# One core, four layers: values joined to the output weights in layer 0, softmax transposes in one row, and another pace of sampling in layer 1

## The chip, the core and the metric

The kernel runs on one core of a Trainium2 chip. A core has a matrix engine (PE), a vector engine (DVE), a scalar engine (ACT), a general one (POOL), one that mostly issues DMAs (SP), and DMA queues. The engines run side by side, each through its own list of instructions in order, and wait for each other by semaphores. The metric is the device time of one execution in microseconds; the median of several runs counts. All data is 32-bit float.

## What is computed

The input `x` has two images of 512 channels with 32 x 32 points (1024). Four layers follow each other:

```python
# layer 0: attention of 1024 points over 64 sampled keys, 8 heads of 64
sim = einsum("bhid,bhjd->bhij", qh, kh) + bias      # bias: a small MLP of point and key
attn = softmax(sim)
out = einsum("bhij,bhjd->bhid", attn, vh)
x = x + einsum("bchw,oc->bohw", out, out_w) + out_b
x = x + mlp_w2 @ gelu(mlp_w1 @ bn(x) + b1) + b2     # 512 -> 2048 -> 512
# layer 1: d = normalised depthwise + pointwise convolution of the lower channels
off = conv(d, off_w)                                # 9 taps, an (y, x) offset each
dc = sum over taps of dc_w[tap] @ bilinear(d, tap + off)
x = x * d * sigmoid(layernorm(dc)) + x * g          # g: a gate from pooled channels
# layer 2: linear attention; layer 3: group norm, 8-head attention, projection
```

## The kernel before

**Order.** The order on PE is the order of the program; a tile scheduler orders DVE, ACT, POOL and SP by itself. `weave`, `some` and `next` step Python generators, and so mix stages by hand into PE's list: each `yield` is a place where another stage may be cut in. A tile pool with n buffers makes a new tile wait until the tile n before it has been read for the last time.

**Layer 0.** `queries_keys_values` makes queries, keys and values at the start. Keys and values are kept in block form, two heads to a block of 128 (`kbd`, `vbd`, L706 to L760). `biased_scores` then fills `simT` in 128 steps: hidden layers `h` (DVE L804, ACT L813), matmuls `ph` (L824), evictions `hi` and `lo` (L834 to L837), the last layer and the scores `sim` (L845), `store` (DVE L867). Pairs 0 to 3 of `simT` belong to image 0, pairs 4 to 7 to image 1. `softmax_values` works pair by pair: eight transposes `pt` (L909), maximum, subtraction, exponential, sum, reciprocal, product (L915 to L922), eight transposes `pb` back (L928), a copy `at` (ACT L934), the product with `vbd` (L940) and its copy into `simT` (DVE L943). `project` (L966) multiplies `simT` by `out_w`. For image 0 this runs alone; for image 1 it is woven into `mlp.run(0)`. `Mlp` has matmuls `ph` (L1026), gelu `h` (ACT L1034) and matmuls `acc` (L1015).

**Layer 1.** `Features` makes `x_pad` (memset on POOL L1079, copy on ACT L1084), the depthwise sums `dw` on DVE (L1092, L1096), `pd` (L1112), `d`, then `d_pad` (memset POOL L1139, copies ACT L1141), offsets `po` (L1153), `pos` (DVE L1165) and indices after `pp` (L1218). `Products` multiplies `d` by each of the 9 taps in 8 blocks: 72 steps per image, called "made" steps, each four matmuls `py` (L1291), a copy `y` (ACT L1299) and a DMA into a table in memory (SP L1300). `Samples` gathers from the finished tables: 72 pairs of indirect DMAs `got` per image (POOL L1343), with four additions `dfacc` on DVE each (L1354). `pools` lists the buffers for `got`; `due` takes one pair if the table of its tap is complete. `gate_image` applies the layer norm and the gate (transposes `pt` L1389, sigmoid `gated` ACT L1395, product L1398, `x_all` DVE L1400).

**How they are joined.** Image 0's products start in `mlp.run(1)`; its gathers go on with two buffers, then four beside image 1's features; `found` is the generator of features. Image 1's gathers go on three buffers while `gate_image(0)` steps once per made step, and on up to five afterwards while `linear.run(0)` and `group_norm_terms` step once per made step. `group_norm_terms` waits on DVE's `spread` for `pvar` (L1605).

**Layer 3.** `att.normalize` makes `h` (ACT L1663) from `x_all`; keys and queries `pq` (L1703) follow. `att.values(0)` makes `v` in 32 steps of one matmul `pv` (L1680), `BESIDE` of them per step of `linear.run(1)` (`pkv` L1550, `pa` L1564, evictions `x_all` L1573). `Attention.heads` then does logits `pl` (L1770), exponentials `e` (ACT L1866), transposes `pt` (L1820), weighing `po` (L1785).

## Time and profile before

| | us |
|---|---|
| median of three runs | 3969.76 |
| lowest and highest of them | 3967.2, 3973.1 |
| profiled execution | 3967.19 |
| its span, first to last instruction | 3965.4 |
| ACT's first exponential of the softmax, with its table (2114.55 to 2117.85) | 3.3 |
| POOL memset of d_pad (128 x 4624) | 3.96 |
| DVE add of a gather (128 x 512, mean of 560) | 0.748 |
| gather, issue to landing, median | 6.7 |
| table block, issue to landing, median | 5.5 |

A row of a timeline reads: start, duration, engine, line, operation, output and inputs with shapes, how often, and in brackets how long the engine sat idle before it and whose result it then had. A matmul of 32-bit floats shows as two records. The next view is of five stretches of the span (busy time of PE, PEld, DVE, ACT and POOL with counts, then granted clock, share of busy DMA engines and rate): the softmax of image 0, the features of image 1, the gate, the linear stage, the end of image 1's products.

```profile
2105.00:2152.00 47.00, 24.07 (x91) 14.14 (x92) 26.77 (x26) 9.57 (x10) 0.06 (x1) 0.78 0.53 221
2839.00:2985.00 146.00, 130.55 (x551) 57.83 (x550) 112.85 (x170) 28.87 (x46) 75.70 (x62) 0.92 0.85 305
2985.00:3125.00 140.00, 135.43 (x330) 60.43 (x328) 108.17 (x180) 29.39 (x52) 66.54 (x60) 0.97 0.90 331
3125.00:3240.00 115.00, 106.39 (x335) 52.06 (x334) 89.94 (x142) 19.59 (x34) 54.37 (x52) 0.96 0.80 292
3240.00:3313.00 73.00, 64.94 (x149) 28.23 (x147) 55.02 (x79) 12.31 (x21) 40.64 (x36) 0.97 0.96 365
```

### The profile page before, as it was taken

To read this page: it belongs to the slowest core of one execution; us is meant where nothing else is said; L and a number is where in the kernel's file an instruction comes from. 1 tells how busy PE (TensorE), PEld (TensorE's weight loads), DVE (VectorE), ACT (ScalarE), POOL (GpSimd) and SP (SyncE) were. 2 spreads that over 40 slices of the span, in tenths; PEclk is the share of its full clock that TensorE was granted. 3 is DMA by queue.
4 is the path that set the end of the run, shared out by engine and by line. 5 is a ranking of instruction groups with operands and counts; after the bars stand their busy time and mean duration, and the time that the engine had idled before them with its cause. 6 is when DMAs were issued, how large, how long until landed. Compare 5 with 4: busy or idle time off the path is not lost. (4 is left out here: it accounts for less than half of the span.)

```text
span 3965.4 us, 59982 instructions
## 1 busy us (share of the span) xinstructions
PE 3847.6 (97%) x25596; PEld 1498.6 (38%) x25596; DVE 2967.5 (75%) x3320; ACT 2536.3 (64%) x2858; POOL 340.7 (9%) x325
## 2 busy tenths in 40 slices
PE   7999999999999999999997999999999999999999
PEld 4322232222322222222333444444344444455555
DVE  7999999999999999999995114044577878666565
ACT  7999999999999999999992211211121212345544
POOL 0000000000000000000000000022354544000000
PEclk9999999999999999999998999999999999999999
DMA  3000000000000000000002000056788987000000
GB/s 106 2 22 22 22 23 1 22 22 23 17 7 22 23 22 3 21 22 22 1 1 106 0 0 24 18 177 198 259 289 320 336 300 256 1 1 11 1 19 25
DMA packets 90479, 274.66 MB, mean 69 GB/s; under 512 B 9140, under 2 KB 10804, under 8 KB 86884
## 3 DMA queue, kind: packets, MB, share of 16 engines
q0 software_dynamic: 42432, 154.39, 11.1%
q1 hardware_dynamic: 47780, 116.44, 8.2%
q8 instruction: 200, 3.28, 0.3%
q14 instruction: 67, 0.55, 0.0%
HBM read 228.59 MB, written 42.21 MB: 68 GB/s over the span
## 5 line engine op out<-in xcount | busy, mean ns | idle before, releaser
L824 PE MATMUL ph<-h,w_t 128*32 128x512 f32 x16384 | 1796.2, 593 | 15.3 <-ACT lo L834 7.0
L804 DVE TENSOR_TENSOR h<-ab 128x1024 f32<-128x1024 f32 x1024 | 1205.5, 1218 | 73.8 <-PE ph L824 72.7
L824 PEld LDWEIGHTS ph<-h,w_t 128*32 128x32 f32 x16384 | 528.8, 110 | 1257.3 <-issue 1079.2
L813 ACT ACTIVATE h<-h 128x1024 f32<-128x1024 f32 x832 | 870.4, 1066 | 45.5 <-DVE h L804 43.4
L837 DVE SCALAR_TENSOR_TENSOR hi<-lo,low_w,hi 128x1024 f32<-128x1024 f32 x512 | 654.6, 1278 | 30.0 <-ACT hi L836 29.3
L836 ACT ACTIVATE hi<-ph,size_b,size 128x1024 f32<-128x1024 f32 x512 | 620.5, 1212 | 15.6 <-PE ph L824 9.6
L834 ACT ACTIVATE lo<-ph,vec_t 128x1024 f32<-128x1024 f32 x512 | 571.2, 1116 | 2.4 <-PE ph L824 2.4
L1354 DVE SCALAR_TENSOR_TENSOR dfacc<-got,wts,dfacc 128x512 f32<-128x512 f32 x560 | 408.5, 748 | 214.9 <-DMA got<-table,idx 206.4
L1291 PE MATMUL py<-dc_w_t,d 128*128 128x512 f32 x1152 | 523.9, 610 | 23.1 <-ACT y L1299 23.1
L1299 ACT COPY y<-py 128x512 f32<-128x512 f32 x144 | 83.6, 584 | 478.3 <-PE py L1291 426.8
L1343 POOL DMA_INDIRECT got<-table,idx x288 | 319.9, 1111 | 501.1 <-DVE dfacc L1354 171.9
L1291 PEld LDWEIGHTS py<-dc_w_t,d 128*128 128x128 f32 x1152 | 221.1, 195 | 302.1 <-issue 269.5
L1866 ACT ACTIVATE e<-pl,m 128x1024 f32<-128x1024 f32 x128 | 143.5, 1121 | 217.1 <-DVE m L1858 217.1
L1858 DVE TENSOR_REDUCE m<-pl 128x1 f32<-128x1024 f32 x128 | 150.8, 1219 | 143.8 <-PE pl L1770 143.8
L845 PE MATMUL sim<-hi,w 128*32 128x512 f32 x2048 | 244.9, 592 | 1.8 <-DVE hi L837 1.8
L1026 PE MATMUL ph<-xn,mlp_w_t 128*128 128x512 f32 x512 | 229.6, 592 | 0.0
L1015 PE MATMUL acc<-h,mlp_w_t 128*128 128x512 f32 x512 | 229.3, 592 | 0.0
L1034 ACT ACTIVATE h<-ph,vec_t 128x512 f32<-128x512 f32 x64 | 44.0, 687 | 254.2 <-PE ph L1026 254.0
L1079 POOL MEMSET x_pad<- 128x1156 f32 x2 | 2.2, 1099 | 2061.5 <-PE ph L824 2061.5
L1820 PE MATMUL pt<-cst_t,e 128*128 128x128 f32 x1024 | 149.6, 279 | 4.8 <-DVE aT L1829 2.7
L1820 PEld LDWEIGHTS pt<-cst_t,e 128*128 128x128 f32 x1024 | 118.9, 142 | 92.4 <-issue 60.2
L1015 PEld LDWEIGHTS acc<-h,mlp_w_t 128*128 128x128 f32 x512 | 97.2, 190 | 122.0 <-issue 122.0
(233 smaller groups left out, 2472.3 us busy)
## 6 DMA issues: line engine op xcount, KB each, us to landing
table<-y SPq DMA_DIRECT2D x144, 256.0 KB, 5.5
ab<-feat_d SPq DMA_DIRECT2D x64, 512.0 KB, 4.4
dc_w_t<-in_dc_w_dram SPq DMA_DIRECT2D x18, 1024.0 KB, 6.2
mlp_w_t<-in_mlp_w_dram SPq DMA_DIRECT2D x2, 4096.0 KB, 16.8
got<-table,idx POOLq DMA_INDIRECT x288, 6.7
w_qkv_t<-in_w_qkv_dram SPq DMA_DIRECT2D x3, 1024.0 KB, 9.1
out_dram<-x_all SPq DMA_DIRECT2D x12, 256.0 KB, 2.0
x_all<-in_x_dram SPq DMA_DIRECT2D x4, 512.0 KB, 8.7
```

Of the source, the lines that this page charges most:

```text
L804: nc.vector.tensor_tensor(h1, at_x[:, k : k + 1, :].to_broadcast([128, 32, 32]), at_y[:, k, :].unsqueeze(2).to_broadcast([128, 32, 32]), A ...
L813: nc.scalar.activation(h1, h1, AF.Relu)
L824: nc.tensor.matmul(ph[32 * t : 32 * t + 32, half(n)], lhsT=w2[:, c0 : c0 + 32], rhs=pair[t // 2][:, half(n)], start=True, stop=True, skip_ ...
L834: nc.scalar.activation(lo, phs[0], AF.Relu, bias=b2_lo)
L836: nc.scalar.activation(hi, phs[1], AF.Relu, bias=size_b, scale=size)
L837: nc.vector.scalar_tensor_tensor(hi, lo, low_w, hi, ALU.mult, ALU.add)
L845: nc.tensor.matmul(sim[32 * t : 32 * t + 32, half(n)], lhsT=w3[:, 30 - j : 62 - j], rhs=sums[t][:, half(n)], start=(j == 0), stop=(j == 30 ...
L1015: nc.tensor.matmul(accs[oc], lhsT=self.w2[:, m, 128 * oc : 128 * oc + 128], rhs=hs[m], start=(m == 0), stop=(m == 15),)
L1291: nc.tensor.matmul(py, lhsT=f.d[:, cc, 128 * c : 128 * c + 128], rhs=w[:, cc, :], start=(cc == 0), stop=(cc == CC - 1),)
L1343: nc.gpsimd.indirect_dma_start(out=g[:, 2 * dy : 2 * dy + 2, :].rearrange("p s c -> p (s c)"), out_offset=None, in_=self.products.tables[f ...
L1354: self.net.nc.vector.scalar_tensor_tensor(acc, g[:, s, :], self.f.wts[:, c, k, s : s + 1], self.f.bias if (k, s) == (0, 0) else acc, ALU.mult,
L1820: nc.tensor.transpose(pt[:, 128 * c : 128 * c + 128], e[:, 128 * k : 128 * k + 128], ident)
```

## The change

- Values are made as block products `val`, one 128 x 128 block per pair of heads, by the loop that makes the keys. A new `projected` multiplies each block by the output weights once (`pm`, eight matmuls of 128 x 512, copied by ACT to `outv`); `project` uses `outv`, and the product with `vbd` and its copies go. Four `pm` stand ahead of image 0's projection, four behind it.
- The softmax of image 0 moves into `biased_scores`: the transposes of pairs 0 and 1 stand ahead of the last `last_layer`, those of pairs 2 and 3 behind it, then four `turn`, and `store` of the last pair comes last. `out_w` and `mlp_w1` are loaded at step 16 of the last pair, into the space of `q_pad`.
- Image 0's `Samples` get three buffers in the MLP of image 1, and one more afterwards; `due` is called there only while i < 30; image 1's features begin two made steps later.
- Image 1's `Samples` have two buffers until image 0's gate is done, then six. The gate takes two steps per made step; `linear.run(0)` steps in two of three made steps.
- `values(0)` of layer 3 takes 19 steps beside `linear.run(1)`, and the other 13 in `heads`, behind the first logits.

```diff
@@ -167,7 +163,7 @@
...
-        "vw": vw_stack,
+        "vw": _pair_blocks(np.asarray(i["L0_conv_vw"])),
...
@@ -292,46 +289,70 @@
         scores = ExitStack()
         sim_pool = net.pool(scores, "l0_sim", side="right")
         simT = sim_pool.tile([128, NP, HW], F32, name="simT", tag="simT")
-        vbd = sim_pool.tile([128, NP, 128], F32, name="vbd", tag="vbd")
+        val = sim_pool.tile([128, NP, 128], F32, name="val", tag="val")
+        room = ExitStack()
+        big = net.pool(room, "l0_q")
+        def new_room():
+            return big.tile([128, 4 * 2048 + CC * C], F32, name="room", tag="room")
         with ExitStack() as l0a:
             l0a.enter_context(net.tc.manual_schedule(engines={mybir.EngineType.PE}))
-            big = net.pool(l0a, "l0_q")
-            q_flat = big.tile([128, (NP * 36 + 6) * 34], F32, name="q_pad", tag="q_pad")
+            q_flat = new_room()[:, : (NP * 36 + 6) * 34]
...
             first = net.pool(l0a, "cpb_ab", 4)
-            parts = queries_keys_values(net, bn, simT, q_flat, q_pad, kbd, vbd, feat, first)
+            parts = queries_keys_values(net, bn, simT, q_flat, q_pad, kbd, val, feat, first)
...
-            biased_scores(net, q_pad, kbd, feat, w2, simT, first, parts)
+            def load_weights():
+                t = new_room()
+                w1 = t[:, : 4 * 2048].rearrange("p (k m) -> p k m", m=2048)
+                out_w = t[:, 4 * 2048 :].rearrange("p (k m) -> p k m", m=C)
+                nc.sync.dma_start(out=out_w, in_=net.ins["out_w"])
+                nc.sync.dma_start(out=w1, in_=net.ins["mlp_w1"])
+                return w1, out_w
+            w1, out_w = biased_scores(
+                net, q_pad, kbd, feat, w2, simT, first, parts, load_weights
+            )
         later.enter_context(net.tc.manual_schedule(engines={mybir.EngineType.PE}))
         dram = net.pool(later, "l1_dram", space=bass.MemoryType.DRAM)
         image0 = ExitStack()
-        with ExitStack() as l0b:
-            mlp = Mlp(net, l0b, s2)
-            out_w = net.load("out_w", net.pool(scores, "out_w", side="right"))
-            soft = net.pool(scores, "att_tmp", 2, side="right")
-            with ExitStack() as ctx:
-                ps = net.psum(ctx, "att_ps", 4)
-                for _ in softmax_values(net, 0, simT, vbd, soft, ps):
-                    pass
+        with room, ExitStack() as l0b:
+            mlp = Mlp(net, l0b, s2, w1)
+            soft = net.pool(scores, "att_tmp", side="right")
             mlp.open_psum(l0b)
             with ExitStack() as ctx:
                 ps = net.psum(ctx, "att_ps1", 1)
-                project(net, 0, simT, out_w, mlp.bank)
-                weave(mlp.run(0), softmax_values(net, 1, simT, vbd, soft, ps), 1, 3)
-                project(net, 1, simT, out_w, mlp.bank)
+                def two_banks(name):
+                    return ps.tile([128, HW], F32, name=name, tag="two")
+                def one(name, size):
+                    return soft.tile([128, size], F32, name=name, tag=name, bufs=2)
+                made = projected(net, val, out_w, soft, mlp.bank)
+                some(made, CC - 1)
+                outv = next(made)
+                project(net, 0, simT, outv, mlp.bank)
+                some(made, 99)
+                weave(mlp.run(0), Softmax(net, simT, one, two_banks).image(1), 1, 3)
+                project(net, 1, simT, outv, mlp.bank)
...
             with ExitStack() as ctx:
-                banks["turn"] = net.psum(ctx, "ft_ps", 2)
+                banks["turn"] = net.psum(ctx, "ft_ps", 2), "turn"
...
                 taken = None
@@ -339,18 +360,19 @@
                     some(found, FOUND[i] if i < len(FOUND) else 0)
                     if i == len(FOUND):
                         some(found, 99)
-                        sums0 = Samples(net, f0, products, own0, 2, side="right")
+                        sums0 = Samples(net, f0, products, own0, 3, side="right")
                         taken = sums0.run()
                     if i >= MADE:
                         for _ in range(2):
                             next(made)
-                            if taken is not None:
+                            if taken is not None and i < 30:
                                 sums0.due(taken)
...
             linear = Linear(net, l2)
             own1 = ExitStack()
             f1 = Features(net, 1, own1)
-            more = net.pool(own1, "df_more", 2)
-            sums0.pools += [more, more]
+            more = net.pool(own1, "df_more", 1)
+            sums0.pools += [more]
             found = f1.run(bank, True)
             for i, _ in enumerate(made):
-                some(found, 2)
+                if i > 1:
+                    some(found, 2)
                 if i % 4 < 3:
                     sums0.due(taken)
             some(found, 99)
             sums1 = Samples(net, f1, products, own1, 1)
-            sums1.pools += [more, more]
+            sums1.pools += [more]
             tmp = net.pool(own1, "df_tmp", 1)
             made = products.run(f1, turn)
             taken1 = sums1.run()
-            aside = None
+            aside, ctx2 = None, None
             for i, _ in enumerate(made):
-                if i == 62:
-                    sums1.pools = sums1.pools[:3]
                 if aside is None:
                     if next(taken, None) is None:
                         aside = gate_image(net, f0, sums0, tmp, bank)
                         wait = i + 4
-                else:
-                    sums1.due(taken1)
-                    if i >= wait and next(aside, None) == "gated":
-                        own0.close()
-                        ctx2 = ExitStack()
-                        extra = net.pool(ctx2, "df_extra", 2, side="right")
-                        sums1.pools += [extra, extra]
-                        linear.open(ctx2, side="right")
-                        aside = chain(
-                            linear.run(0, bank, kv_bank),
-                            group_norm_terms(net, linear.tmp, 0, bank),
-                        )
+                    continue
+                sums1.due(taken1)
+                if ctx2 is None and i >= wait:
+                    if next(aside) != "gated" and next(aside) != "gated":
+                        continue
+                    own0.close()
+                    ctx2 = ExitStack()
+                    linear.open(ctx2, side="right")
+                    extra = net.pool(own1, "df_extra", 4)
+                    sums1.pools += [extra] * 4
+                    aside = chain(
+                        linear.run(0, bank, kv_bank),
+                        group_norm_terms(net, linear.tmp, 0, bank),
+                    )
+                elif ctx2 is not None and i % 3 < 2:
+                    next(aside, None)
             for _ in aside:
                 next(taken1, None)
             ctx2.close()
@@ -415,9 +440,8 @@
                 values = att.values(0, turn)
                 for i, _ in enumerate(linear.run(1, bank, kv_bank)):
                     some(values, BESIDE[i])
-                some(values, 99)
             l2.close()
-        layer3(net, att, later, out)
+        layer3(net, att, later, values, banks, out)
@@ -427,7 +451,7 @@
-BESIDE = (1, 3, 2, 2, 2, 2, 2, 2, 2, 2, 3, 3, 2, 2, 1, 1)
+BESIDE = (1, 2, 1, 1, 1, 1, 1, 1, 1, 1, 3, 3, 1, 1, 0, 0)
...
@@ -727,42 +750,30 @@
...
+            for w, out, factor in ((kw, kbd, 64**-0.5), (vw, val, 1.0)):
+                for q in range(2):
+                    pk = bank("pk")
+                    for c in range(4):
+                        nc.tensor.matmul(
+                            pk[:, 128 * c : 128 * c + 128],
+                            lhsT=w[:, c, :],
+                            rhs=kvbd[:, 4 * q + c, :],
+                            start=True,
+                            stop=True,
+                        )
+                    nc.vector.tensor_scalar(
+                        out[:, 4 * q : 4 * q + 4, :],
+                        pk.rearrange("p (c j) -> p c j", j=128),
+                        factor,
+                        None,
+                        ALU.mult,
+                    )
     return done
-def biased_scores(net, q_pad, kbd, feat, w2, simT, first, parts):
+def biased_scores(net, q_pad, kbd, feat, w2, simT, first, parts, load_weights):
...
@@ -890,73 +901,95 @@
...
             elif j == 16:
                 scores(p, sim)
+                if p == NP - 1:
+                    weights = load_weights()
             pending = (p, j, sums)
+        def two_banks(name):
+            return ps_h.tile([128, HW], F32, name=name, tag="ph")
+        def one(name, size):
+            if size == HW:
+                pool, tag = (hid1, "h1") if name == "e" else (highs, "hi")
+                return pool.tile([128, HW], F32, name=name, tag=tag)
+            return small.tile([128, size], F32, name=name, tag=f"soft_{name}", bufs=2)
+        soft = Softmax(net, simT, one, two_banks)
+        es = [soft.attention(p) for p in range(2)]
         last_layer(sim, *pending[1:])
+        es += [soft.attention(p) for p in range(2, CC)]
+        for p, e in enumerate(es):
+            soft.turn(p, e)
         store(NP - 1, sim)
...
+        return weights
+class Softmax:
+    def __init__(self, net, simT, one, banks):
+        self.net, self.simT, self.one, self.banks = net, simT, one, banks
+    def attention(self, p):
...
+    def turn(self, p, e):
+        pb = self.banks("pb")
         for c in range(8):
...
+            self.net.nc.tensor.transpose(
                 pb[:, 128 * c : 128 * c + 128],
                 e[:, 2 * c : 2 * c + 2, :].rearrange("p h j -> p (h j)"),
...
+                self.net.cst("ident"),
+            )
+        self.net.nc.scalar.copy(self.simT[:, p, :], pb)
+    def image(self, b):
+        first = CC * b
+        ahead = self.attention(first)
+        yield
+        for p in range(first, first + CC):
+            now = ahead
+            if p + 1 < first + CC:
+                ahead = self.attention(p + 1)
+                yield
+            self.turn(p, now)
             yield
...
+def projected(net, val, out_w, pool, bank):
+    nc = net.nc
+    out = pool.tile([128, NP, C], F32, name="outv", tag="outv")
+    for p in range(NP):
+        pm = bank("pm")
+        nc.tensor.matmul(pm, lhsT=val[:, p, :], rhs=out_w[:, p % CC, :], start=True, stop=True)
+        nc.scalar.copy(out[:, p, :], pm)
+        yield out
+def project(net, b, simT, outv, bank):
     nc, x = net.nc, net.x
     for oc in range(CC):
@@ -965,7 +998,7 @@
...
-                    lhsT=out_w[:, k, 128 * oc : 128 * oc + 128],
+                    lhsT=outv[:, CC * b + k, 128 * oc : 128 * oc + 128],
                     rhs=simT[:, CC * b + k, half(n)],
                     start=(k == 0),
                     stop=(k == CC - 1),
...
@@ -1801,6 +1834,8 @@
         ahead = [self.exponentials(*part) for part in logits(*work[0])]
         for e in ahead:
             self.divide(*e)
+        for _ in first:
+            pass
         for at, (b, hp, s0) in enumerate(work):
             now, ahead = [e for e, _ in ahead], []
             if at + 1 < len(work):
...
-    att.heads(first + second, fill)
+    banks["turn"] = att.ps_t, "pt3"
+    att.heads(first + second, values, fill)
     for _ in att.project(1, 768, 256, out, att.last_bank):
         pass
```

## What it will do to the time, predicted before it ran

> **What bounds the kernel now.** I read the busy shares first, then the slices.
>
> ```profile
> span 3965.4 us, 59982 instructions
> PE 3847.6 (97%) x25596; PEld 1498.6 (38%) x25596; DVE 2967.5 (75%) x3320; ACT 2536.3 (64%) x2858; POOL 340.7 (9%) x325
> ...
> PE   7999999999999999999997999999999999999999
> ...
> PEclk9999999999999999999998999999999999999999
> ```
>
> TensorE is busy 97% of the span; 3965.4 - 3847.6 = 118 us is all the idle time there is. So an edit gains in two ways: PE work removed, or a PE wait removed, with the slow matmuls after the wait. The slice row shows one hole behind the start, near 2100 us. The third view is PE's waits, by producer (us in total, times, longest):
>
> ```profile
> PE py L1291 <- ACT y L1299: 23.1, 10, 9.4
> PE pb L928 <- DVE e L922: 14.1, 2, 9.0
> ...
> PE pq L1703 <- ACT h L1663: 8.2, 1, 8.2
> ...
> PE po L940 <- ACT at L934: 4.5, 4, 1.2
> ...
> PE pvar L1605 <- DVE spread L1602: 3.6, 1, 3.6
> ...
> PE pl L1770 <- ACT e L1866: 2.7, 1, 2.7
> ```
>
> The fourth is PE's timeline where those waits are: the softmax of image 0, then the deformable stage (start, duration, group, idle before it and releaser).
>
> ```profile
> 2106.49 1.90 PE L845 MATMUL sim<-hi,w 128*32 128x512 f32 x10 [1.79 <-DVE hi L837]
> 2109.87 1.94 PE L909 MATMUL pt<-cst_t,simT 128*128 128x128 f32 x16 [1.47 <-DVE simT L867]
> 2120.76 1.97 PE L928 MATMUL pb<-cst_t,e 128*128 128x128 f32 x8 [8.95 <-DVE e L922]
> 2123.83 3.78 PE L940 MATMUL po<-at,vbd 128*128 128x512 f32 x4 [1.10 <-ACT at L934]
> ...
> 2133.19 1.04 PE L909 MATMUL pt<-cst_t,simT 128*128 128x128 f32 x8
> 2139.41 1.79 PE L928 MATMUL pb<-cst_t,e 128*128 128x128 f32 x8 [5.18 <-DVE e L922]
> ...
> 2148.37 1.98 PE L940 MATMUL po<-at,vbd 128*128 128x512 f32 x4 [1.16 <-ACT at L934]
> ```
>
> ```profile
> 2873.20 12.38 PE L1291 MATMUL py<-dc_w_t,d 128*128 128x512 f32 x24 [9.44 <-ACT y L1299]
> ...
> 2932.26 10.12 PE L1291 MATMUL py<-dc_w_t,d 128*128 128x512 f32 x16 [3.70 <-ACT y L1299]
> ...
> 3098.26 8.83 PE L1291 MATMUL py<-dc_w_t,d 128*128 128x512 f32 x16 [2.00 <-ACT y L1299]
> ```
>
> A 128x512 matmul is two records; four records take 1.98 us warm and 3.78 cold, spacing 0.86 us per matmul warm. A wait is paid twice: 16 records at 2932.26 take 10.12 us against 7.03 elsewhere.
>
> **The change, part by part**, against the profiled run (3967.19 us, span 3965.4).
>
> 1. *Values and weights of layer 0.* At the start 8 matmuls of 128x64 become 8 of 128x128, and two strided copies (0.69 us each) become two evictions like the keys'; the memset of `vbd` on POOL goes. PE then waits 4.2 us for the first h at 88.0 anyway. **-0.5** (-1 to +0.5).
>
> 2. *Softmax of image 0.* Now PE passes L909, L928, L940 in a chain with DVE and ACT, and projects at 2151.67. In the changed order the logit transposes of pairs 0 and 1 stand ahead of the last 16 `sim` records, at about 2103.7, and no product follows. DVE becomes the chain: from 2104.7 it has 16 operations of 1.18 (maximum, subtract, sum, multiply of four pairs), four reciprocals of 0.2, one `hi` and one `store` of 1.28 each: 18.9 + 0.8 + 2.6 = 22.3, so the last multiply ends by 2127.0. ACT's exponentials (1.0, and 1.28 of table) hide in it: DVE has other pairs to do. Then the last eight transposes, cold, 1.8 (2128.8), the copy 1.0 and its handover (2130.1); the four `pm` matmuls wait for that bank: two cold at 1.8, two at 0.9, 5.4, and projection starts at about 2135.8. **-16** (-12 to -18).
>  Here a rule speaks against the change. The Trainium skill, "TensorE: Matmul & The Clock Gate", section "Part 4: PE-mode transpose", says that transposes do not count as PE activity for the clock. A row of 64 transposes would then leave the clock low, all four `pm` would be cold (+1.8) and the first projection too (+1.7): -12.5. The rows say that transposes do run at full rate between matmuls (1.04 us for eight at 2133.19, 1.79 after a wait of 5.18), but none shows a long row of them alone. I take the row, because DVE's waits, not the rate of transposes, set this stretch; the rule's value is inside the range.
>  Loads: `out_w` and `mlp_w1` are issued some 110 us earlier, behind the last `ab` load on SP, into space that q_pad gave back; `mlp_w2` (4 MB, 16.8 us from issue to landing) is needed in the MLP, some 40 us later. Without the early issue `out_w` would stand behind 8 MB and projection would wait past 2133.
>
> 3. *Image 1.* Its 8 product matmuls leave the MLP stage and 4 `pm` enter it, with a copy each on ACT. That stage shows no idle PE, so work counts in full: -8 x 0.86 + 4 x 0.86 = **-3.5** (-3 to -4). ACT's h (0.69 each, 254 us idle before them in sum) covers the copies.
>
> 4. *Rest in image 0's sums (three buffers, four `due` fewer, features of image 1 two `made` steps later).* At 2873 the wait of 9.44 is ACT: its x_pad copy stands in order behind `dw`, `dw` on DVE behind adds and the last MLP eviction (2843.89, though PE's last `acc` ended at 2839), which stood behind gathers. With fewer adds ahead and a third buffer, the eviction comes 3 to 5 us earlier, adds no longer wait between the nine `dw`, and a sixth product covers instead of five: first half ready near 2862 against PE's need near 2866. Gone with the wait are 1.9 of slow matmuls; late next is the second half, which had slack. **-9.5** (-4 to -11.5).
>  At 2932 the wait is POOL's d_pad memset (3.96 us), queued behind gathers on POOL. The change moves it past three more pairs, but features come two products (7 us) later and their table is there sooner; ACT's copies end about 11 us after the last `pd` against a need at 14. **-5** (-6.8 to 0). `pos` on DVE stands behind five more pairs: 0 to +2, in item 5's range.
>
> 5. *Gate and linear stage.* Image 1 has two `got` buffers (three before) until the gate is done, then six. Queued behind an add that waits are, on DVE, the gate's multiplies and evictions; behind those ACT's sigmoid and y copies; then PE. A buffer's cycle is second issue 1.24 + landing + adds 3.0; two in flight make a pair cost half. Before the gate ends, 11 pairs of image 1 must be through; they begin about 48 us after pp and their limit is about 111. The same skill, "DMA: Bandwidth & Descriptors", section "Anatomy of one DMA", gives 2.0 us plus bytes over 436 GB/s: a gather here is 154.39 MB / 288 = 536 KB, so 3.2 us, 3.7 us per pair, done at 48 + 41 = 89 (estimate): no wait. The rows have 5.7 us of landing in the light stretch, 7.5 here, at most 10.2: 5.0, 5.9 and 7.2 per pair, done at 103, 113, 127: nothing, 2, or 16 late. The row decides: the queues are 90% busy here. Against it, joining two gate steps per product and linear steps at two of three should remove part of the waits 2.26, 2.00, 2.53, 1.19 and their cold matmuls. DVE is the limit next: 40 pairs x 3.0 + 25 of linear is 145 us beside 140 of PE. pvar's 3.6 stays. Sum **+1** (-8 to +12).
>
> 6. *h, 8.16 at 3313.* It waits for the last gather: last y DMA issued at 3305.6, landed 6.1 later. Neither moves against PE: **-0.3** (0 to -1).
>
> 7. *Values of layer 3.* 13 of 32 `pv` (0.86 each) move behind the first logits. They cover the 2.73 for `e`, but had covered the evictions of `pa`, so the first `pl` waits about 4 instead of 1.09: **0** (-4 to +3).
>
> Sum: -0.5 - 16 - 3.5 - 9.5 - 5 + 1 - 0.3 + 0 = **-33.8**: 3933.4 beside the profiled 3967.2. That run is the lowest of three; from the median 3969.8 the same sum gives **3936**.
>
> **The rivals.**
> A. *Only layer 0 gains* (items 1 to 3, -20): in the deformable stage the waits move from ACT's copies to DVE, whose work is unchanged. For: DVE is behind gathers there and 77% busy from 2839 to 2985. Against: it idles for gathers between 2836 and 2860, which the rest removes. **3950**. Chance 0.22.
> B. *The joins work as well*: gate and linear -12 instead of +1, logits -4: -33.8 - 13 - 4 = -50.8, **3919**. For: six buffers after the gate. Against: the two before it. Chance 0.21.
> C. *Slower: two buffers starve the gate.* Place: adds of image 1 on DVE ahead of the gate's evictions. With pairs at 9.5 us (landing near 15) eleven end at 48 + 105 = 153, 42 late, plus 2 cold: -34.8 + 44 is about +9: **3979**. It decides from (111 - 48 + 34.8) / 11 = 8.9 us per pair. Against: no gather took over 10.2 in 3036 to 3095. Chance 0.05.
> D. *The change doesn't do what it says:* transposes of image 0 are early on PE, but the weights land late and projection waits where it did. Against: SP is idle from the last `ab` load to 2104. About 3952; chance 0.02.
>
> **How the numbers follow.** Forecast 3936, chance 0.50, its own range 3926 to 3946. All ends of the costs together give -54 to -4, 3916 to 3966; A and B end inside. I take 3915 to 3959, which leaves out C and the tails of the others. Within 0.2% (8 us, what a measurement can tell from no change) needs over 3962: C is the slower side at 0.05 and other tails 0.01; between them 0.03; faster 0.91.
>
> **What would show each step.** Item 2: `po` of projection starts about 30 us after the last `sim` records, not 45, its wait is for ACT's copy, and the four `pm` ahead take 5 to 6 us. Item 3: 16 `pm` records in all, no po from `at`. Item 4: no py wait over 3 us between the end of the MLP and pp. Item 5: py waits on ACT between pp and pqk, and the length of waits of `dfacc` for `got`; over 10 us in one py wait is C. Item 7: pl waiting for x_all near 4, for e near none. Wrong altogether: PE idle staying above 100 us, or projection not nearer to `sim`.

## The result, and the profile after

The changed kernel takes 3950.47 us (median of 5 runs, 3946.2 to 3952.8) beside 3969.76 us of the kernel before: a ratio of 0.9951, interval 0.9937 to 0.9966, so 19.3 us less. Measured again in another session, in the fifth run below, it was 0.9959 (0.9946 to 0.9973), 19.5 us less. The forecast was 33.8 us less, or 3936. The time of rival A, which gives the gain to layer 0 alone, was 3950.

The page of the changed kernel, busy shares and slices, and then the waits of PE:

```profile
span 3947.6 us, 60251 instructions
PE 3837.4 (97%) x25580; PEld 1516.4 (38%) x25580; DVE 2951.5 (75%) x3312; ACT 2539.7 (64%) x2866; POOL 347.9 (9%) x324
...
PE   7999999999999999999998999999898999999999
```

```profile
PE py L1324 <- ACT y L1332: 24.8, 10, 8.5
PE pb L959 <- DVE e L952: 9.4, 4, 3.3
...
PE pvar L1638 <- DVE spread L1635: 7.7, 1, 7.7
PE pq L1736 <- ACT h L1696: 7.4, 1, 7.4
...
PE pp L1251 <- DVE pos L1198: 5.4, 1, 5.4
...
PE pl L1803 <- DVE x_all L1606: 3.2, 1, 3.2
```

The hole near 2100 us has closed from 7 to 8 in slice 21 (counted from 0). New digits under 9 stand at slices 28 (2763 to 2862 us) and 30 (2961 to 3059), in the deformable stage. `po` waiting for `at` is gone and `pb` waits for less; but `py` waits as long as before (24.8 against 23.1), `pvar` and `pp` longer (7.7 against 3.6, 5.4 against 2.0). PE's timeline shows layer 0:

```profile
2103.34 1.97 PE L939 MATMUL pt<-cst_t,simT 128*128 128x128 f32 x16
...
2106.94 1.90 PE L856 MATMUL sim<-hi,w 128*32 128x512 f32 x10 [0.65 <-DVE hi L848]
...
2125.97 1.94 PE L959 MATMUL pb<-cst_t,e 128*128 128x128 f32 x8 [0.73 <-DVE e L952]
2129.01 6.39 PE L987 MATMUL pm<-room,val 128*128 128x512 f32 x8 [1.10 <-ACT simT L964]
2135.24 15.22 PE L999 MATMUL po<-simT,outv 128*128 128x512 f32 x35
```

Projection starts at 2135.24, 16.4 us before the 2151.67 of the old kernel. The last `acc` of image 1's MLP ends at 2819.6 instead of 2839.2: 19.6 us ahead. Up to here the change does what the steps of the sum for layer 0 (items 1 to 3) say.

Then half of the lead is lost and most of that is won back. `pp` ends at 2976.95 instead of 2980.06. By the change's order two products more lie ahead of it (6.9 us), so at equal work the lead is 10.0 us. At `pq` it is 16.6 (3296.47 against 3313.10), at the end 17.8. In the features of image 1 these are the waits of the changed kernel:

```profile
2831.90 17.43 PE L1324 MATMUL py<-dc_w_t,d 128*128 128x512 f32 x40 [2.02 <-ACT y L1332]
2857.88 15.79 PE L1324 MATMUL py<-dc_w_t,d 128*128 128x512 f32 x32 [8.55 <-ACT y L1332]
...
2926.49 8.75 PE L1324 MATMUL py<-dc_w_t,d 128*128 128x512 f32 x16 [2.77 <-ACT y L1332]
...
2975.02 1.93 PE L1251 MATMUL pp<-cst_t,pos 18*128 18x18 f32 x8 [5.45 <-DVE pos L1198]
```

The wait that was to go (9.44) is there with 8.55, and the one for `pos` is longer. The next view looks at DVE over the stretch from the end of image 1's MLP to the end of its last product, first in the kernel before, then in the changed one. The first row has the busy time of PE, PEld, DVE, ACT and POOL, then granted clock, DMA share and rate; the second has what DVE waited for (in total, times, longest).

```profile
2839.00:3305.00 466.00, 437.30 (x1361) 198.55 (x1359) 359.48 (x559) 88.38 (x149) 232.21 (x204) 0.96 0.87 318
DVE dfacc L1354 <- DMA got<-table,idx: 100.7, 52, 16.4
```

```profile
2819.60:3289.00 469.40, 432.50 (x1360) 197.44 (x1359) 367.39 (x573) 87.30 (x149) 242.46 (x206) 0.96 0.84 313
DVE dfacc L1387 <- DMA got<-table,idx: 97.2, 43, 18.5
```

Add busy and waiting: 359.5 + 100.7 = 460.2 of 466.0 before, 367.4 + 97.2 = 464.6 of 469.4 after. DVE is either working or waiting for a gather in 99% of this stretch, and PE is busy in 92 to 94% of it. This alone doesn't say that DVE sets the length, because gathers wait for others in turn. POOL, which issues them, has these rows in the same two stretches, before and after:

```profile
POOL got L1343 <- DMA table<-y: 40.9, 4, 19.1
```

```profile
POOL got L1376 <- DMA table<-y: 36.2, 3, 27.5
```

In these waits a gather stood until a block of the table had landed, and the tables are filled by PE's own products `py`. DVE's longest wait in the changed kernel, 18.52 us up to 3001.50, is for gathers issued from 2996.19 on, right behind the 27.51 us wait for a table. So PE, ACT, POOL and DVE hold each other here. The change took no addition out of DVE's list (560 records in both pages).

### The profile page after: what moved, and what is told of

It reads as the page before. It is cut to its first block, busy times and chain, and to the rows that moved or that the text cites. A ratio compares the mean times of both kernels' runs of the same rounds, so it can differ in the third digit from the quotient of the medians.

```text
span 3947.6 us, 60251 instructions
## 1 busy us (share of the span) xinstructions
PE 3837.4 (97%) x25580; PEld 1516.4 (38%) x25580; DVE 2951.5 (75%) x3312; ACT 2539.7 (64%) x2866; POOL 347.9 (9%) x324
## 4 chain that ended last, share of the span: by engine, by line
PE 76%; ACT 10%; DVE 6%; DMA 4%; issue 2%; POOL 1%; SPq 0%; POOLq 0%; ACTq 0%; DVEq 0%
PE ph L835 36%; PE py L1324 6%; PE ph L1059 5%; PE acc L1048 5%; PE sim L856 4%; ACT h L824 3%; PE pl L1803 3%; DVE dfacc L1387 3%; DMA got<-table,idx 3%; PE pq L1736 3%; PE po L1818 3%; PE pt L1855 3%; ACT hi L847 2%; ACT lo L845 2%; ACT ab L480 2%
## 5 line engine op out<-in xcount | busy, mean ns | idle before, releaser
L835 PEld LDWEIGHTS ph<-h,w_t 128*32 128x32 f32 x16384 | 547.5, 110 | 1238.2 <-issue 1066.3
L847 ACT ACTIVATE hi<-ph,size_b,size 128x1024 f32<-128x1024 f32 x512 | 620.4, 1212 | 16.3 <-PE ph L835 10.5
L1324 PE MATMUL py<-dc_w_t,d 128*128 128x512 f32 x1152 | 519.4, 606 | 24.8 <-ACT y L1332 24.8
L1376 POOL DMA_INDIRECT got<-table,idx x288 | 328.0, 1139 | 459.1 <-DVE dfacc L1387 152.4
L1059 PE MATMUL ph<-xn,room 128*128 128x512 f32 x512 | 229.6, 592 | 0.0
## 6 DMA issues: line engine op xcount, KB each, us to landing
room<-in_mlp_w_dram SPq DMA_DIRECT2D x1, 4096.0 KB, 15.6
```

The source lines that it names most:

```text
L835: nc.tensor.matmul(ph[32 * t : 32 * t + 32, half(n)], lhsT=w2[:, c0 : c0 + 32], rhs=pair[t // 2][:, half(n)], start=True, stop=True, skip_ ...
L847: nc.scalar.activation(hi, phs[1], AF.Relu, bias=size_b, scale=size)
L1059: nc.tensor.matmul(ph, lhsT=self.w1[:, k, 128 * m : 128 * m + 128], rhs=xn[:, k, :], start=(k == 0), stop=(k == CC - 1),)
L1324: nc.tensor.matmul(py, lhsT=f.d[:, cc, 128 * c : 128 * c + 128], rhs=w[:, cc, :], start=(cc == 0), stop=(cc == CC - 1),)
```

## The experiments

One number for each traced run serves below: the **stretch**, from the end of the last `acc` of image 1's MLP to the start of the first `pq` behind its wait for `h`. The last column is DVE's, from the same start to the end of image 1's last product, 7 to 9 us ahead of that `pq`. Both are of one execution.

The runs were made in five sessions: before and changed; e1 to e4; e5 to e8; e9 to e11; e12. The kernel before took 3969.8, 3977.0, 3978.3, 3966.7 and 3971.0 us in them (medians). A ratio is to the kernel before in its own session; its interval is at 95%, and it need not be the quotient of the medians. All traces of e1 to e8, and none of the other six, have waits of PE that the trace gives no cause for (2 to 24 us in sum from 2820 us on), so the stretch is best compared inside a session.

| kernel | ratio to before (interval) | project at | stretch | DVE busy + waits for gathers |
|---|---|---|---|---|
| before | 1 | 2151.7 | 473.9 | 359.5 + 100.7 |
| changed | 0.9951 (0.9937, 0.9966) | 2135.2 | 476.9 | 367.4 + 97.2 |
| e1 layer 0 only | 0.9925 (0.9909, 0.9942) | 2136.8 | 469.8 | 360.6 + 87.9 |
| e2 old rest | 0.9943 (0.9926, 0.9959) | 2133.2 | 470.8 | 363.4 + 86.7 |
| e3 quiet | 0.9985 (0.9978, 0.9992) | 2136.7 | 494.7 | 351.9 + 80.9 |
| e4 old heads | 0.9954 (0.9937, 0.9970) | 2133.3 | 485.2 | 365.5 + 93.0 |
| e5 changed again | 0.9959 (0.9946, 0.9973) | 2134.4 | 481.6 | 367.8 + 91.0 |
| e6 no layer 0 | 1.0023 (1.0012, 1.0033) | 2153.0 | 486.8 | 365.7 + 96.0 |
| e7 no delay | 0.9925 (0.9910, 0.9940) | 2134.3 | 484.0 | 365.6 + 83.9 |
| e8 due to the end | 0.9957 (0.9942, 0.9973) | 2132.7 | 491.2 | 366.3 + 92.2 |
| e9 late softmax | 0.9961 (0.9948, 0.9975) | 2142.9 | 467.0 | 359.0 + 89.3 |
| e10 layer 0 and heads | 0.9938 (0.9924, 0.9951) | 2134.0 | 467.5 | 363.7 + 84.4 |
| e11 three until gate | 0.9935 (0.9919, 0.9950) | 2134.2 | 463.4 | 364.8 + 84.5 |
| e12 delay alone | 0.9929 (0.9915, 0.9942) | 2133.0 | 465.0 | 366.4 + 83.4 |

**e1.** Both images' sampling, the gate, the linear steps and the heads set back in the changed kernel (the core of it):

```diff
-                        sums0 = Samples(net, f0, products, own0, 3, side="right")
+                        sums0 = Samples(net, f0, products, own0, 2, side="right")
...
-            sums1.pools += [more]
+            sums1.pools += [more, more]
```

> Only layer 0 is changed (values and weights joined, softmax of image 0 early, weights loaded early); sampling, gate, linear stage and heads are as before. My theory, read from the two traces: the changed kernel projects 16.4 us earlier and finishes image 0's and image 1's MLP 19.9 us earlier, and the layers behind it only pass this on. So this kernel takes 3969.8 - 20 = 3950 us, as the changed one, and its first py of the features of image 1 waits 8 to 10 us as before. Rival: the earlier arrival is lost here too because the sampling of image 0 then runs closer to its tables; then it stays above 3956.

Measured 3947.9 beside 3977.0: 29 us less, 23 to 36 by the interval, more than the 20 expected. Beside the first session's trace of the kernel before, this one is 18.1 us ahead at the end of the MLP (2821.1 against 2839.2) and 22.2 at `pq`. Where the rest lies is not shown, as there is no trace of the kernel before from the session of e1. The wait of 8 to 10 us that was expected to stay did not (0.8 is left): the first half's `dw` waited for no gather in this execution. So layer 0 alone gives at least the whole gain.

**e6.** The counterpart: layer 0 of the kernel before, and everything else of the change. Against the kernel before:

```diff
-                        sums0 = Samples(net, f0, products, own0, 2, side="right")
+                        sums0 = Samples(net, f0, products, own0, 3, side="right")
...
-                some(found, 2)
+                if i > 1:
+                    some(found, 2)
...
-            sums1.pools += [more, more]
+            sums1.pools += [more]
```

> Layer 0 as before; the rest in the sums, the joined gate and linear steps and the split values of layer 3 as in the changed kernel. Theory: these edits together gain nothing, since the rest costs 7 to 10 us in image 1's features (DVE has 17 more additions ahead of pp) and the gate and heads give back 6 and 1: 3966 to 3972 beside a before of 3970, ratio 0.999 to 1.001. Rival: they gain by themselves and layer 0 less than 20: ratio under 0.997.

3985.5 beside 3978.2: 7.2 us slower, where no difference was expected, and the interval (5 to 13 us) leaves out no change. -29 and +7 make -22, near the -19.5 of both together: the change is one gain, less one loss.

**e5.** The changed kernel once more, with no edit, for the others to be compared with.

> The changed kernel once more, as the measure beside the next ones. 0.9951 of the kernel before, as in its first runs; if the spread of single runs (waits without a releaser on PE while gathers run) is what moves it, between 0.993 and 0.997.

0.9959, in the range of the spread: the gain repeats.

**e2.** The rest undone, the joins kept:

```diff
-            more = net.pool(own1, "df_more", 1)
-            sums0.pools += [more]
+            more = net.pool(own1, "df_more", 2)
+            sums0.pools += [more, more]
...
-                if i > 1:
-                    some(found, 2)
+                some(found, 2)
```

> The changed kernel with the pace of image 0's sums as before: two buffers then four, due called to the end of the MLP, features of image 1 from the first made step on. Image 1 still has two buffers up to the gate (later five instead of six, for lack of space), and the gate and linear steps stay joined. Theory A: the rested sums cost 10 us in the features of image 1 and the joins gain 6 us in the gate and linear stage by themselves: 3940 us, and the pp of image 1 comes some 20 us before that of the kernel before. Theory B: the gain in the gate stage only comes from additions that the rest had pushed out of it into the features' stage; then undoing the rest moves both back and the time stays at 3950.

3953.8 by the median of four, 3942.8 to 3955.5. The ratio, 0.9943, would be 3947 in the first session: between both theories. The traced execution is the fastest of the four and goes with theory A: `pp` came 23.0 us before that of the kernel before, and `pq` 24.7. The other three, at 3952 to 3956, have no trace. Yet even this execution lost some 14 us at one place behind `pp`. These are ACT, DVE and PE there, one fence for each timeline:

```profile
3055.36 0.59 ACT L1331 COPY y<-py 128x512 f32<-128x512 f32 x1 [0.96 <-ACT gated L1427]
3071.39 0.78 ACT L1427 ACTIVATE gated<-pt,vec_t 128x512 f32<-128x512 f32 x1 [15.45 <-DVE x_all L1432]
```

```profile
3069.88 0.75 DVE L1386 SCALAR_TENSOR_TENSOR dfacc<-got,wts,dfacc 128x512 f32<-128x512 f32 x1 [3.86 <-DMA got<-table,idx]
3070.55 0.75 DVE L1432 SCALAR_TENSOR_TENSOR x_all<-gated,gate,x_all 128x512 f32<-128x512 f32 x1
```

```profile
3074.62 6.73 PE L1323 MATMUL py<-dc_w_t,d 128*128 128x512 f32 x8 [10.73 <-ACT y L1331]
```

From the bottom up: PE waits 10.73 us for a copy of `y`; the copy stands behind ACT's sigmoid, which waits 15.45 for a buffer that DVE's `x_all` frees; `x_all` stands in DVE's order behind additions, of which the last has a gather that has not landed. It is the mechanism of rival C, at a lower price: the PE wait is 10.73, and eight records take 6.73 instead of 3.60 after it.

**e11.** The same with three buffers for image 1:

```diff
-            sums1.pools += [more]
+            sums1.pools += [more, more]
```

> As e2_old_rest, but image 1's sums have three buffers until the gate instead of two. In e2 PE waited 10.7 us at 3074.6 for y copies, ACT's sigmoid 15.5 us for DVE's evictions of the gate, and DVE stood in order behind an addition whose gather had not landed. Theory: two buffers are the cause; with three that wait falls to 0 to 4 us and the time falls 6 to 9 us below e2 (0.9943 to about 0.992 to 0.993). Rival: the joined gate steps are the cause, as they ask for evictions twice as fast; then the wait stays near 10 us.

The PE wait at that place is 3.52, as the theory says, and the stretch is 7.4 us shorter, though in another session. The times (0.9935 and 0.9943) overlap and don't separate the two by themselves. What DVE waits for gathers between `pp` and the first `pqk`, within 2 us of it, shows the buffers best; the kernel before (three buffers), the changed one (two), e2 (two), e11 (three):

```profile
DVE dfacc L1354 <- DMA got<-table,idx: 30.6, 16, 16.4
```

```profile
DVE dfacc L1387 <- DMA got<-table,idx: 43.1, 13, 18.5
```

```profile
DVE dfacc L1386 <- DMA got<-table,idx: 39.5, 18, 12.7
```

```profile
DVE dfacc L1386 <- DMA got<-table,idx: 23.9, 15, 12.4
```

The longest wait of each row, 12 to 19 us, is the one for a table and is there with two and with three buffers. Between e2 and e11, which differ by the buffer alone, two buffers cost DVE 15.6 us of waiting in this part. Over the whole stretch hardly anything of that is left (86.7 against 84.5). In the changed kernel PE shows little of it there (1.2 and 3.3). Its longer wait at `pvar` (7.7) isn't shown to be the buffers' price: e2, also with two, has 1.2, and e11 2.9.

**e12.** The two steps' delay put into e11, alone:

```diff
-                some(found, 2)
+                if i > 1:
+                    some(found, 2)
```

> As e11_three_until_gate, and only the delay of image 1's features by two made steps put back. Theory: the delay puts two steps' gathers and additions of image 0 ahead of the features in the order of POOL and DVE. The depthwise operations start later after the MLP's last eviction (4 us in the traces with the delay), wait about 5 us for gathers, and the py wait of 8 us at the second x_pad copy returns: 0.9935 becomes 0.995 to 0.996. Rival: the loss of the rest in the changed kernel came from its buffers or the fewer due; then this stays at 0.993 to 0.994 and that py wait stays under 2 us.

The mechanism came as expected and the time did not follow. The trace of e12 has the wait:

```profile
2859.76 13.44 PE L1324 MATMUL py<-dc_w_t,d 128*128 128x512 f32 x24 [9.84 <-ACT y L1332]
```

It is 9.84 us with 2.9 us of slow matmuls behind it (13.44 against 10.57 for the same 24 records in e11), and e12 is 0.9929 where e11 is 0.9935, with intervals of 5 to 6 us to each side. Its stretch is 465.0 against 463.4: what PE lost here was back before `pq`. DVE's two terms are the same in both kernels (449.8 and 449.3). That fits a length set by DVE and its gathers and doesn't prove it: e7, in a session with waits that have no cause in the trace, has 449.5 and a stretch of 484.0.

**e7.** The delay taken from the changed kernel:

```diff
-                if i > 1:
-                    some(found, 2)
+                some(found, 2)
```

> The changed kernel, but image 1's features begin with the first made step again; three buffers and four due fewer stay. Theory: the cost of the rest is additions pushed into the features' stage, not the delay: pos stands behind some five additions fewer, because the stage is two made steps shorter, and the time falls by 0 to 4 us from the changed one. Rival: the delay was the cover for the copies of x_pad; without it the waits of 2 and 8.6 us become longer and it takes 4 us more.

3949.2 beside 3958.7 of the changed kernel in the same session; the intervals don't overlap, so this is faster than the changed kernel, by some 9 us, more than expected. The py wait of 8 us fell to 1.1. Its traced execution (3955.9) is the slowest of its four and lost the gain behind `pp`, so it doesn't show where the 9 us come from. The delay costs something here and nothing between e11 and e12. The two pairs differ in image 1's buffers (two here, three there), in the rest of image 0's sums and in session; which of these makes the difference is open.

**e8.** `due` to the end of the MLP:

```diff
-                            if taken is not None and i < 30:
+                            if taken is not None:
```

> The changed kernel with due called to the end of the MLP of image 1; three buffers and the delay stay. DVE sat idle from 2779.7 to 2813.9 in the changed kernel, room for eleven pairs. Theory: four pairs go back into it, DVE has 12 us less to do in the features' stage, and the wait of pp for pos (5.5) and of py for rstd (3.5 and 1.6) go: 5 to 10 us less than the changed kernel, if the additions do not delay the last eviction of the MLP. Rival: they stand ahead of that eviction in DVE's order, x_pad comes 6 to 9 us later, and nothing is gained.

0.9957, as the changed kernel. The last evictions began 6.4 us after the last `acc` in both, against 4.7 before the change: the four missing `due` made them no earlier. In both traces six additions in a row stand right ahead of them in DVE's list.

**e3.** No gather of image 0 in the first 11 made steps of the features:

```diff
-                if i % 4 < 3:
+                if i % 4 < 3 and not 0 <= i < 11:
```

> The changed kernel, but no gather of image 0 is taken in the first 11 made steps of image 1's features, so that no addition stands between the 18 depthwise operations on DVE. Theory: the waits of 2.0 and 8.6 us and the 1.9 us of slow matmuls behind them go (-12); eight pairs of additions (24 us of DVE) move behind, where DVE has 15 to 20 us spare up to the pp, so 2 to 10 us come back there: 3940 to 3948. Rival: the bound is DVE's sum over the whole stage and everything comes back: 3950 or more.

The rival is right, and more: the wait of 8.6 us went (1.08 is left), and the kernel became slower than the changed one, 0.9985 by 20 runs. The work that was put off came back: PE waited 11.2 us at `pvar`, and DVE 29.0 us for ACT's sigmoid. So the very wait that the prediction set out to remove could go, and time was lost. How much of the loss the work put off accounts for is not shown: the traced execution is the slowest of the 20, and it has 24 us of PE waits without a cause in the trace.

**e4.** Values of layer 3 as before:

```diff
-BESIDE = (1, 2, 1, 1, 1, 1, 1, 1, 1, 1, 3, 3, 1, 1, 0, 0)
+BESIDE = (1, 3, 2, 2, 2, 2, 2, 2, 2, 2, 3, 3, 2, 2, 1, 1)
...
+                some(values, 99)
```

> The changed kernel with the values of layer 3 as before: all 32 steps beside the linear stage of image 1 and none in the heads. From the traces, layer 3 took 1.2 us less after the change: pl's waits of 1.1 and 2.7 us became one of 3.2. So this takes 3951 to 3952 us, and the pl waits of 1.1 and 2.7 us are back. Rival: the values moved nothing: 3950, which cannot be told apart by the time, only by the waits.

0.9954; the time can't tell it from the changed kernel. The `pl` waits of 1.1 and 2.7 us are back in place of 3.2.

**e9 and e10.** In e9 the softmax of image 0 runs behind the scores, without the product; e10 is e1 with the split values. e9 against e1:

```diff
-        es = [soft.attention(p) for p in range(2)]
         last_layer(sim, *pending[1:])
-        es += [soft.attention(p) for p in range(2, CC)]
-        for p, e in enumerate(es):
-            soft.turn(p, e)
...
+                ps4 = net.psum(ctx, "att_ps", 4)
...
+                for _ in Softmax(net, simT, one, four).image(0):
+                    pass
```

> As e1_layer0_only, but the softmax of image 0 stands where it stood before the change, behind the scores, with four pairs of banks and no product; the values joined to the output weights and the early loads stay. Theory: in layer 0 the gain splits: the products and their evictions leave the chain, but the last pairs still wait for DVE, so projection starts some 8 to 10 us before 2151.7 instead of 16; the placing of the first two pairs ahead of the last scores gives the other 6 to 8. Time 6 to 8 us over e1, about 3956 to 3958 if e1 is 3950. Rival: removing the products gives nearly all of it and this is within 2 us of e1.

> Layer 0 and the split values of layer 3 as in the changed kernel; the sums, gate and linear steps as before. Theory: the sums' rest and delay and the joins cost 7 to 10 us together, so this is as fast as e1 or 1 to 2 us faster: 0.992 to 0.993 of the kernel before, faster than both the kernel before and the changed kernel (0.9951 and 0.9959). Rival: the joins are needed with the heads' split: 0.995.

e9 projects at 2142.9: 8.7 us of the 16.4 come from the chain without products, 7.7 from the early place. In time e9 is 14 us under its kernel before, and e1 29 us under its own; the theory had 6 to 8 between them, and what makes up the rest is not shown. e10, in e9's session, is 10.5 us under e9. It is 0.9938, its interval holding e1's value: the split is not worth anything that these times show. That e10 is faster than the changed kernel, as was expected, the intervals don't show.

## Why the prediction was right and where it was wrong

The measured time lies in the forecast's range, and the part of the sum that names layer 0 came as worked out. The part for the deformable stage did not, and that the range held is in part luck: 3950 is the time of rival A, which was counted in. One of the forecast's own signs of being wrong altogether came true as well: PE's idle time was to fall below 100 us and is 3947.6 - 3837.4 = 110.2.

- *Item 1*, -0.5: the first `ph` behind the start came at 87.27 instead of 87.98, -0.7. Of this 0.4 was left at the last but one group of `sim` (2094.64 against 2095.08).
- *Item 2*, -16: projection is 16.4 earlier, 16.0 without that 0.4. DVE's chain was as worked out: the last eight transposes at 2125.97 where 2127.0 was reckoned (of the forecast's own times, 2130.1 and 5.4 make 2135.5 and not 2135.8). The four `pm` took 6.2 us, between 5.4 (two of them cold) and 7.2 (all cold). The rule on transposes (the Trainium skill, "TensorE: Matmul & The Clock Gate", section "Part 4: PE-mode transpose") would have made it -12.5, with every `pm` and the projection cold; it was right for part. The granted clock was 1.00 from 2103.3 to 2110.8, where 32 transposes of logits stand beside the last `sim`. It was 0.59 from 2110.8 to 2129.0, where four groups of eight transposes each stand behind a wait for DVE, 0.56 during `pm`, and 1.00 in the first 15 us of projection. Whether the waits or the transposes lowered it these rows can't tell.
- *Item 3*, -3.5: the end of the MLP moved by 19.6, so -3.2.
- *Item 4*, -9.5 and -5: this step failed. At equal work the features' stage became 9.6 us longer (157.4 - 6.9 = 150.5 against 140.9), and the sign that was named, no py wait over 3 us, did not come (8.55 and 3.50). The step had three premises. That the last eviction would come 3 to 5 us earlier: 6.4 us after `acc` instead of 4.7 (e8). That a sixth product covers: five copies of `y` stood between the x_pad copies in every kernel. That the gathers would not hold DVE between the `dw`: in the changed kernel they did, for 4.2 us and for 1.1 right ahead. There the delay puts two steps' gathers ahead of POOL's memset and of `dw`. In all six traces with the delay and without e3's quiet the PE wait is 7.3 to 14.2 us; without the delay it is at most 1.1, but for the kernel before, where it was 9.4.
- Behind these lies the real fault: I read PE's waits as separate and removable, in a stretch where PE, ACT, POOL and DVE hold each other. In e12 a PE wait of 9.8 us was put in and cost nothing that the times show. In e3 one of 8.6 was taken out and gained nothing, though e3 moved other work too.
- *Items 5 and 6*, +1 and -0.3: at equal work `pp` to `pq` took 6.6 us less. The two buffers did starve (43.1 us of DVE's waits against 30.6, of which 18.5 and 16.4 are the wait for a table). So the row of landing times was the right one to take. The wrong one was the price of 3.2 us per gather, estimated from the skill's "DMA: Bandwidth & Descriptors", section "Anatomy of one DMA": the median landing was 7.0. What gave time back is argued, not shown: the features' stage had taken 27 additions more ahead of `pp` (126 against 99; e6's expectation says 17), work moved and not saved.
- *Item 7*, 0: -1.2, with waits of 3.2 for the evictions and none for `e`, as named.

In sum: -19.6 by layer 0 where -20 was forecast; +3.0 for the whole stretch where items 4 to 6 had -13.8; -1.2 in layer 3. Rival A had the number, and its ground in part: DVE's additions are unchanged. But the waits on ACT's copies did not move to DVE. They stayed (21.7 us in the stretch before, 23.4 after), and those for DVE at `pp` and `pvar` grew from 5.6 to 13.1. Its number is luck in part too, since by e1 and e6 it is a larger gain less a loss.

e1, e7, e10, e11 and e12 are all faster than the kernel before, with 0.9925 to 0.9938. e7 is clear of the changed kernel by intervals of one session; the others were not measured beside it.

Open: what sets the length of the stretch; why the delay costs time in e5 against e7 and none in e12 against e11; and how the loss of e6 divides between the rest and the two buffers, as no kernel here has the rest together with three buffers for image 1.

## What to carry to other kernels

Before a wait is put into a sum as removable, add up, for each engine and for the stage, busy time and waits for transfers, and ask of each transfer what it waited for in turn. If the two make the whole stage for one engine, a wait that goes from another engine is likely to come back elsewhere, even if that other has the higher busy share. Here a PE wait could be put in without cost (e12), and one could go while time was lost (e3). Work that was delayed was only moved (126 additions ahead of `pp` instead of 99). The time won in layer 0, on the other hand, where PE waited in a chain with DVE and ACT, was still there at the end (e1).

## What the hardware showed unexpectedly

In the traces of e1 to e8 PE sometimes waited with nothing to release it while gathers ran: 6.1 us once at a `py` of e4, 21 such groups from 2820 us on in e3. The traces of before, changed and e9 to e12 show none. In the two sessions of e1 to e8 the kernel before, too, was slower than in the others (3977.0 and 3978.3 against 3966.7 to 3971.0). Single executions of one kernel differ by up to 15 us there (3951.3 to 3966.0 in e5). What these waits are is not shown.

A gather's issue on POOL, 1.0 us in the median, took 15.4 us once in the changed kernel and 8.7 in the kernel before, each time while `dw` ran on DVE. All traces but e7's have such an issue at that place, of 7.8 to 15.9 us; these runs don't show what held it.
